# Reading the tokens in turned layout and normalizing them there, instead of normalizing and transposing them

## The chip, the core and the metric

The kernel runs on one core of one Trainium2 chip. The metric is the device time of one execution in microseconds. The core has a matrix engine (TensorE, PE in the profile; its weight loads are listed as PEld), a vector engine (VectorE, DVE), a scalar engine (ScalarE, ACT), GpSimd (POOL), and SyncE (SP), which here issues nearly all DMAs. Each engine works through its own instructions in the order in which the program wrote them, and semaphores hold an instruction until what it needs is there.

## What is computed

2048 tokens x of width 512 (32 batches of 64) attend to 2048 context tokens, each batch to its own; then comes a linear layer with a low-rank adapter. Both branches are gated and added back. Cut to what matters:

```python
x = x + tanh(g_xattn[0]) * xattn(layernorm(x), ctx, mask, bias, Wq, Wk, Wv, Wo)
x = x + tanh(g_ffn[0]) * ffn(layernorm(x), weight, bias, lora_A, lora_B, starts)

# layernorm: (x - mean) / sqrt(var + 1e-5), over the 512 features
# xattn: q = h @ Wq; k = ctx @ Wk; v = ctx @ Wv          (32 heads of 128)
#        p = softmax(q k^T / sqrt(128) + bias, masked);  out = (p v) @ Wo
```

The change touches the first layernorm only: its result, turned so that features lie on the partitions and tokens along them, is the operand of q = h @ Wq.

## The kernel before

All products of the projections are float32 made of three matmuls of split operands: a high part (a copy rounded by ACT) and a low part (the remainder, a subtraction). Projections use a seven-product scheme for a 2x2 block product: blocks p1 to p7 of the activations and of the weights are sums and differences of quarters, prepared by ACT (high part) and DVE or POOL (sums and low part).

The work is done in two passes (p = 0, 1) of 1024 tokens. A pass has three stages:

- the key stage: 16 pairs of heads (n = 0 to 15), one `unit` each; a unit is seven products of six matmuls, in the order p1, p6, p7, p5, p2, and, after the next unit's p1, its p4 and p3 (the `carry`). Keys go to DRAM (`kd`). POOL prepares the weight blocks of the next pair (`key_blocks`).
- the value stage: four groups g of four token tiles t, a unit for each, so 16 units. Values go to DRAM (`vd`). During a group POOL prepares the weight blocks of the next one (`blocks_v`) from four loads (`fetch_v`).
- attention, pair by pair: query projection, scores, softmax, product with v, output projection.

Everything beside the matmuls is written as generators ("streams"). After each product the program calls `beat()` (line 64), which takes one step of every stream; `paced(g, k)` takes a step of g every k beats. A unit has seven beats. Thus the order of instructions on every engine is fixed when the program is built; nothing is scheduled later. `drain` runs what is left of a stream.

The tokens come into this as follows. In pair 3 of the key stage `x_stats` starts: it loads the pass's eight tiles of 128 tokens (`x_load`, line 516), tokens on the partitions, and makes mean and variance of each on DVE into `mv` (128 partitions by 8 tiles by 2); `ln_rstd` then makes the reciprocal deviation `y` (128 by 8) in 15 small DVE operations. In pair 9 `x_turns` starts (line 575): it loads each tile a second time, normalizes it in place with one DVE operation (`ln_apply`, line 130), turns it by four transposes on PE into one PSUM tile (`transposes`, line 133), and ACT copies that into f (`x_turn`, line 521). f is two tiles `f0`, `f1` of 128 partitions by 4 by 512: features on the partitions, 512 tokens along each. The same memory held the turned context until pair 2. In group 2 of the value stage `turned_sums`, and in group 3 `turned_blocks`, make the seven blocks of the query projection out of f, on POOL and ACT.

Row buffers of 128 by 512 (pool `rows`) come from a ring of two; the x tiles, the mask tile, the two tiles of `turned_sums` and later the softmax's turned tiles share it. The mask (`mask_stream`, line 591) and in pass 0 the adapter masks (`adapters`, line 471) are made in group 1, and in pass 1 the reciprocal deviations of the finished pass 0 (`acc_rstd`, line 612).

The lines that matter most are the last ones of the key stage and the first ones of the value stage in `stage_a` (line 617), with the functions that it calls:

Of the kernel before, what the change touches and what calls it, by code (L numbers as in the profile page):

```python
# [9 lines left out]
F32 = mybir.dt.float32  # L10
# [4 lines left out]
ALU = mybir.AluOpType  # L15
AX = mybir.AxisListType

P = 128
D = 512
KT = D // P  # L20
# [3 lines left out]
NPH = 2  # L24
TP = NB * S // NPH
NCH = TP // 512
NT = TP // P
# [13 lines left out]


@with_exitstack
def flamingo_block(ctx: ExitStack, tc: tile.TileContext, x, ctxT, bias, mask, gx, gf,
                   wq, wk, wv, wo, wffn, bffn, la, lb, starts, out):
    nc = tc.nc
    PS = bass.MemoryType.PSUM
# [6 lines left out]
    rows = ctx.enter_context(tc.tile_pool(name="rows", bufs=2))  # L54
    st = ctx.enter_context(tc.tile_pool(name="st", bufs=2))
    dram = ctx.enter_context(tc.tile_pool(name="dram", bufs=1, space=bass.MemoryType.DRAM))
# [5 lines left out]
    streams = []  # L62
# [6 lines left out]
    def drain(g):  # L69
        if g in streams:  # L70
            streams.remove(g)
            for _ in g:
                pass
# [2 lines left out]
    make_identity(nc, ident)  # L76
    x1d = dram.tile([NT * P, D], F32, name="x1d")
    kd = [[dram.tile([P, 2, TP], F32, name=f"kd{p}_{n}") for n in range(NPR)] for p in range(NPH)]
    vd = [[dram.tile([P, NT, 512], F32, name=f"vd{p}_{g}") for g in range(2 * NG)] for p in range(NPH)]

    def big(tag, shape, dt, name):
        return slot.tile(shape, dt, tag=tag, name=name)

    def psum(name, shape=(P, 512)):
        return psp.tile(list(shape), F32, tag="ps", name=name)
# [44 lines left out]
    def ln_apply(xn, xt, mv, y, t):  # L130
        nc.vector.tensor_scalar(xn, xt, mv[:, t, 0:1], y[:, t:t + 1], ALU.subtract, ALU.mult)

    def transposes(xn, nm):
        ps = psum(f"tp{nm}", (P, KT, P))
        for kt in range(KT):
            nc.tensor.transpose(ps[:, kt, :], xn[:, kt * P:(kt + 1) * P], ident)
        return ps
# [16 lines left out]
    def sum_blocks(f, tags, nm, eng, out):  # L154
        b11, b21, b12, b22 = parts(f)
        t2 = [rows.tile([P, 512], F32, tag="row", name=f"{nm}t2_{kt}") for kt in range(2)]

        def sub(o, a, b):
            for kt in range(2):
                eng.tensor_tensor(o[kt], a[kt], b[kt], ALU.subtract)  # L160

        sub(b11, b12, b11)
        yield
        sub(b12, b22, b12)
        yield
        sub(t2, b22, b11)
        yield
        out["p6"] = act_block("p6", t2, tags, nm, eng)
        yield
        out["p7"] = act_block("p7", b12, tags, nm, eng)  # L170
        yield
        out["p5"] = act_block("p5", b11, tags, nm, eng)
        yield
        sub(b21, b21, t2)
        yield
        out["p4"] = act_block("p4", b21, tags, nm, eng)
# [275 lines left out]
    f = [big(f"f{j}", [P, KT, 512], F32, f"c0_{j}") for j in range(2)]  # L452
# [63 lines left out]
    def x_load(p, t, nm):  # L516
        xt = rows.tile([P, D], F32, tag="row", name=f"{nm}{p}_{t}")
        nc.sync.dma_start(out=xt, in_=x[p * NT + t])
        return xt

    def x_turn(xt, f, p, t):
        ps = transposes(xt, f"x{p}_{t}")
        nc.scalar.copy(f[t // 4][:, :, (t % 4) * P:(t % 4 + 1) * P], ps)

    V_ORDER = [None] * 5 + ("s3 s3 p1 p1 s2 s2 s1 p6 p6 s1 p7 p7 s4 p5 p5 p2 p2 s4 p4 p4 p3 p3").split()
    K_ORDER = "s3 s3 p1 p1 s2 s2 s1 s1 p6 p6 p5 p5 p7 p7 p2 p2 s4 s4 p4 p4 p3 p3".split()

    def paced(g, k):
        for _ in g:
            yield  # L530
            for _ in range(k - 1):
                yield
# [39 lines left out]
        mvx[p] = mv  # L572
        yield from ln_rstd(mv, f"x{p}", rx, p)

    def x_turns(p, f):
        mv, y = mvx[p], rx[p]
        xt = x_load(p, 0, "xt")
        for t in range(NT):
            nx = x_load(p, t + 1, "xt") if t + 1 < NT else None
            for _ in range(2):  # L580
                yield
            ln_apply(xt, xt, mv, y, t)
            for _ in range(3):
                yield
            x_turn(xt, f, p, t)
            xt = nx
            yield

    masks = {}

# [21 lines left out]
    def acc_rstd(p):  # L612
        for c in range(p * NCH, (p + 1) * NCH):
            yield from ln_rstd(mv2[:, c * 4:(c + 1) * 4, :], f"f{c}", rstd, c, 5)
            yield

    def stage_a(p, first, fc, res, rot, more, enter, kt0):
        xc, plain = first
        f = None
        for n in range(NPR):  # L620
            g = p * NPR + n
            if n == 0:
                sums = sum_blocks(fc, res, f"c{p}", nc.vector, xc)
                streams.append(sums)
            if n == 1:
                keys = key_blocks(p)
                streams.append(keys)
            if n == 3:
                f = [big(f"f{j}", [P, KT, 512], F32, f"xf{p}_{j}") for j in range(2)]
                t7 = big(rot[7], [P, 2, 1024], F32, f"wvr{p}_0a")  # L630
                t8 = big(rot[8], [P, 2, 1024], F32, f"wvr{p}_0b")
                fetch_v(p, 0, [t7[:, 0], t7[:, 1], t8[:, 0], t8[:, 1]])
                if more:
                    streams.append(paced(more, 2))
                xstat = x_stats(p)
                streams.append(xstat)
            if n == 5:
                vsum = [None] + [rwp.tile([P, 1024], F32, tag=f"r{2 + i}", name=f"vs{p}_0_{i}") for i in range(2)] + [None]
                v0 = paced(blocks_v(p, 0, rot, vsum, nc.vector, K_ORDER), 3)
                streams.append(v0)  # L640
            if n == 9:
                drain(xstat)
                xturn = x_turns(p, f)
                streams.append(xturn)
            kt = kt0 if n == 0 and kt0 else k_tile(g)
            w = wt[("k", g)]

            def store(kt=kt, n=n):
                for i in range(2):
                    nc.sync.dma_start(out=kd[p][n][:, i, :], in_=kt[:, i, :])  # L650
            if n < 2:
                for j in range(1 if kt is kt0 else 0, 2):
                    plain_half(w, plain, k_dst(kt), f"k{g}", j)
                store()
            else:
                if n == 2:
                    drain(sums)
                carry[:] = [unit(w, xc, None, k_dst(kt), f"k{g}", tuple(carry)), store]
        drain(xturn)
        drain(v0)  # L660
        xq = {}
        for g in range(NG):
            if g == 1:
                streams.append(mask_stream(p))
                if p:
                    streams.append(acc_rstd(p - 1))
                if p == 0:
                    streams.append(adapt)
            if g == NG - 1:
                t4 = pieces(rwp.tile([P, 1024], F32, tag="r1", name=f"x{p}t4"))  # L670
                fetch("q", p * NPR, "r0")
                bias = enter()
                streams.append(turned_blocks(f, [rot[(7 * NG + i) % 9] for i in range(7)], f"x{p}", nc.gpsimd, keep,
                                             t4, xq, bias, enter))
            for t in range(4):
                if t == 1:
                    if g + 1 < NG:
                        raw = [rwp.tile([P, 1024], F32, tag=f"r{i}", name=f"wvr{p}_{g + 1}_{i}") for i in range(4)]
                        fetch_v(p, g + 1, raw)
                        streams.append(blocks_v(p, g + 1, rot, None, nc.gpsimd, V_ORDER))  # L680
                    if g == NG - 2:
                        keep = {}
                        streams.append(turned_sums(f, f"x{p}", nc.gpsimd, keep))
                if t == 2 and g == NG - 1:
                    streams.append(prep("q", p * NPR, nc.gpsimd))
                vt = kqp.tile([P, 4, 512], F32, tag="kq", name=f"vt{p}_{g}_{t}")
                dst = {(i, j): vt[:, i * 2 + j, :] for i in range(2) for j in range(2)}
                after = unit(wt["v", p, g], xc, slice(t * P, (t + 1) * P), dst, f"v{p}_{g}_{t}", tuple(carry))

                def store(vt=vt, g=g, t=t):  # L690
                    for i in range(2):
                        for j in range(2):
                            nc.sync.dma_start(out=vd[p][2 * g + i][:, j * 4 + t, :], in_=vt[:, i * 2 + j, :])
                carry[:] = [after, store]
        enter()
        return xq
# [342 lines left out]
    for p in range(NPH):  # L1039
# [4 lines left out]
        if p < NPH - 1:  # L1044
            f, gate = [], []
# [119 lines left out]
```

## Time and profile before

| What | Value |
|---|---|
| median of 3 runs | 1545.6 us (1545.55 to 1545.87) |
| the profiled execution's own time | 1545.82 us |
| its span (first to last instruction) | 1543.8 us |
| granted TensorE clock | 1.00 |
| key stage of pass 0: start of pxk groups of pairs 8 and 9 | 90.94 and 100.90 us |
| mean DMA rate | 160 GB/s |
| DMA queue of SP and ACT (q1) | 43.6% of 16 engines |

The span counts from the first to the last recorded instruction; the time of the execution has some 2 us more around it. In a list of groups each line gives the source line, the engine, the operation, what it writes and reads by the program's names, its shape, and how often. A tile view gives the shortest, median and longest duration in ns. In the chain and in a timeline the first column is the start in us, the second the duration in us. A name such as pxk is the PSUM tile "px" of a key unit, pxv of a value unit; wk7p is a weight block of pair 7, wv_1p one of value group 1. A releaser ("<- ACT ...") is what a waiting instruction waited for.

### The profile page before, as it was taken

How to read it: one execution, taken by the hardware profiler on the slowest of the kernel's cores; microseconds unless marked ns; L12 is line 12 of the kernel's file. 1: busy time of each engine (PE TensorE's matmuls, PEld its weight loads, DVE VectorE, ACT ScalarE, POOL GpSimd, SP SyncE). 2: the span in 40 equal slices, each digit the busy share in tenths (PEclk: the TensorE clock that was granted, in tenths of full speed). 3: DMA queues.
4: the chain of work that ended last, by engine and by line, in shares of the span. 5: the costliest groups of instructions: out<-in, count | busy, mean ns of one | idle time of the engine just before them, and what ended most of it. 6: DMA issues, size and time to landing. Idle time of an engine off the chain costs nothing.

```text
span 1543.8 us, 24975 instructions
## 1 busy us (share of the span) xinstructions
PE 1535.5 (99%) x9064; PEld 1292.2 (84%) x9064; DVE 948.3 (61%) x1579; ACT 730.8 (47%) x1610; POOL 1015.8 (66%) x1128
## 2 busy tenths in 40 slices
PE   9999999999999999999999999999999999999999
PEld 7888888888888888888888888888888888888887
DVE  5665343377676757575686535437767675757774
ACT  6454233345555555556445423334555555555621
POOL 3898378967665757575589837896766575757410
PEclk9999999999999999999999999999999999999999
DMA  5654444374243424531565544437424342444211
GB/s 207 243 191 177 165 171 164 137 280 177 83 177 136 163 87 177 190 141 67 213 222 191 178 170 166 164 136 282 176 83 178 137 158 94 174 189 147 80 42 69
DMA packets 80989, 246.37 MB, mean 160 GB/s; under 512 B 9857, under 2 KB 10881, under 8 KB 72674
## 3 DMA queue, kind: packets, MB, share of 16 engines
q1 hardware_dynamic: 80578, 244.26, 43.6%
q8 instruction: 71, 1.16, 0.3%
q10 hardware_dynamic: 288, 0.52, 0.1%
q14 instruction: 52, 0.43, 0.1%
HBM read 171.35 MB, written 73.40 MB: 159 GB/s over the span
## 4 chain that ended last, share of the span: by engine, by line
PE 95%; DMA 2%; DVE 2%; POOL 0%; issue 0%; ACT 0%; SPq 0%; DVEq 0%; POOLq 0%; ACTq 0%
PE pa L97 22%; PE po L818 7%; PE pzv L97 6%; PE pvv L97 6%; PE pxv L97 6%; PE pxq L97 5%; PE pzq L97 5%; PE pxk L97 5%; PE pzk L97 5%; PE pvk L97 5%; PE pvq L97 5%; PE ps L760 4%; PE ppk L97 3%; PE pyv L97 3%; PE pf L97 3%; PE pyk L97 2%
## 5 line engine op out<-in xcount | busy, mean ns | idle before, releaser
L97 PE MATMUL pa<-wo,ch 128*128 128x512 f32 x1024 | 319.9, 393 | 0.0
L793 ACT COPY pt<-tp 32x256 f32<-32x256 f32 x496 | 200.3, 404 | 87.7 <-DVE tp L776 76.6
L89 POOL TENSOR_TENSOR wo<-rawo,wo 128x512 fp32r<-128x512 f32 x64 | 81.1, 1286 | 223.3 <-ACT wo L88 215.5
L97 PEld LDWEIGHTS pa<-wo,ch 128*128 128x128 f32 x1024 | 189.4, 188 | 40.0
L842 DVE TENSOR_TENSOR acc<-pa,acc 128x512 f32<-128x512 f32 x256 | 170.0, 673 | 79.4 <-PE pa L97 79.3
L97 PE MATMUL pa<-wo,cl 128*128 128x512 f32 x512 | 199.7, 390 | 0.0
L818 PEld LDWEIGHTS po<-pt,v 128*128 128x128 f32 x1024 | 119.1, 192 | 2.6 <-ACT pt L793 0.2
L822 DVE TENSOR_TENSOR cl<-po,ch 128x512 fp32r<-128x512 f32 x128 | 88.3, 692 | 52.5 <-ACT ch L821 52.0
L818 PE MATMUL po<-pt,v 128*128 128x128 f32 x1024 | 119.4, 275 | 0.0
L97 PEld LDWEIGHTS pa<-wo,cl 128*128 128x128 f32 x512 | 96.1, 188 | 20.7
L353 DVE TENSOR_TENSOR vt<-pvv,vt 128x512 f32<-128x512 f32 x64 | 44.1, 690 | 111.9 <-PE pvv L97 111.9
L821 ACT CAST ch<-po 128x512 fp32r<-128x512 f32 x128 | 74.8, 586 | 71.5 <-PE po L818 70.9
L766 ACT ACTIVATE sm<-sm 128x512 f32<-128x512 f32 x64 | 40.6, 634 | 123.2 <-POOL sm L765 123.2
L765 POOL TENSOR_TENSOR sm<-sm,mx 128x512 f32<-128x512 f32 x64 | 66.9, 1048 | 46.8 <-DVE mx L764 46.8
L375 ACT COPY vt<-pxv 128x512 f32<-128x512 f32 x32 | 18.8, 588 | 132.1 <-PE pxv L97 132.1
L353 DVE TENSOR_TENSOR kT<-pvk,kT 128x512 f32<-128x512 f32 x56 | 38.5, 688 | 67.1 <-PE pvk L97 66.7
L721 POOL TENSOR_TENSOR sm<-sm,madd 128x512 f32<-128x512 f32 x60 | 76.3, 1292 | 2.6 <-DMA sm<-bias 2.6
L784 POOL TENSOR_TENSOR sm<-sm,r 128x512 f32<-128x512 f32 x64 | 66.8, 1044 | 14.5 <-DVE r L783 11.1
L353 DVE TENSOR_TENSOR qT<-pzq,qT 128x512 f32<-128x512 f32 x64 | 44.3, 692 | 38.0 <-PE pzq L97 37.4
L760 PE MATMUL ps<-kB,qT 128*64 128x64 f32 x2048 | 67.2, 224 | 0.3 <-DVE qT L353 0.3
L353 DVE TENSOR_TENSOR vt<-pzv,vt 128x512 f32<-128x512 f32 x64 | 44.2, 691 | 37.1 <-PE pzv L97 36.9
L760 PEld LDWEIGHTS ps<-kB,qT 128*64 128x64 f32 x2048 | 62.5, 138 | 4.9 <-issue 0.7
(978 smaller groups left out, 3704.0 us busy)
## 6 DMA issues: line engine op xcount, KB each, us to landing
kd<-kT SPq DMA_DIRECT2D x64, 512.0 KB, 3.6
vd<-vt SPq DMA_DIRECT2D x128, 256.0 KB, 2.3
kB<-kd SPq DMA_DIRECT2D x32, 1024.0 KB, 4.9
v<-vd SPq DMA_DIRECT2D x32, 1024.0 KB, 8.7
rawq<-wq SPq DMA_DIRECT2D x32, 512.0 KB, 4.0
sm<-bias SPq DMA_DIRECT2D x64, 256.0 KB, 5.3
rawo<-wo SPq DMA_DIRECT2D x32, 512.0 KB, 3.4
rawk<-wk SPq DMA_DIRECT2D x31, 512.0 KB, 5.4
```

What stands on the lines that cost most here:

```text
L89: eng.tensor_tensor(lo, raw, hi.bitcast(F32), ALU.subtract)
L97: nc.tensor.matmul(ps, a, b, start=start and i == 0, stop=stop and i == 3 * n - 1, skip_group_check=True)
L353: nc.vector.tensor_tensor(o, ps, i, ALU.add)
L721: nc.gpsimd.tensor_tensor(t, t, masks[p][0], ALU.add)
L760: nc.tensor.matmul(ps[h * S:(h + 1) * S, t, :], qT[:, i, tok], kT[:, i, tok], start=True, stop=True)
L765: nc.gpsimd.tensor_tensor(s, s, mx.unsqueeze(2).to_broadcast([P, NT, S]), ALU.subtract)
L784: nc.gpsimd.tensor_tensor(ss[i], ss[i], r.unsqueeze(2).to_broadcast([P, NT, S]), ALU.mult)
L793: f(pt[dst, i, :, src], of[src, :, ki * 32:(ki + 1) * 32])
L818: nc.tensor.matmul(ps[:, t * P:(t + 1) * P], b["v", n // 2][c][:, t, hg * P:(hg + 1) * P], pt[:, i, c * 4 + t, :], start=True, stop=True)
L821: nc.scalar.copy(ch[:, i, sl], ps)
L822: nc.vector.tensor_tensor(cl[:, i, sl], ps, ch[:, i, sl].bitcast(F32), ALU.subtract)
L842: nc.vector.tensor_tensor(acc[t], ps, acc[t], ALU.add)
```

## The change

The host passes x a second time, as `xT`, in the layout of f. Two loads per pair in pairs 6 to 9 put the raw, turned tokens into f. In pair 10 `x_spread` stores the means and the reciprocal deviations to DRAM, so that they lie in the order of the tokens there (`lnd`, two rows of 1024 numbers; partition q of tile t goes to place t*128 + q). From the start of the value stage `x_norm`, at one step in two beats, loads 512 means and 512 deviations at a time onto all partitions and normalizes f in place on DVE: a subtraction and a multiplication for each of the eight rows of 512. The second loads of x, `ln_apply` on them, the transposes and ACT's copies are gone from this place. `mask_stream` and `adapters` start in group 2 instead of group 1, `acc_rstd` stays in group 1.

```diff
+    lnd = [dram.tile([2, TP], F32, name=f"lnd{p}") for p in range(NPH)]
...
-    def x_turn(xt, f, p, t):
-        ps = transposes(xt, f"x{p}_{t}")
-        nc.scalar.copy(f[t // 4][:, :, (t % 4) * P:(t % 4 + 1) * P], ps)
...
-    def x_turns(p, f):
+    def x_spread(p):
         mv, y = mvx[p], rx[p]
-        xt = x_load(p, 0, "xt")
-        for t in range(NT):
-            nx = x_load(p, t + 1, "xt") if t + 1 < NT else None
-            for _ in range(2):
-                yield
-            ln_apply(xt, xt, mv, y, t)
+        nc.sync.dma_start(out=lnd[p][0].rearrange("(t q) -> q t", q=P), in_=mv[:, :, 0])
+        nc.sync.dma_start(out=lnd[p][1].rearrange("(t q) -> q t", q=P), in_=y)
+
+    def x_norm(p, f):
+        for j in range(NCH):
+            row = [rows.tile([P, 512], F32, tag="row", name=f"ln{p}_{j}_{i}") for i in range(2)]
+            for i in range(2):
+                nc.sync.dma_start(out=row[i], in_=lnd[p][i][j * 512:(j + 1) * 512].partition_broadcast(P))
             for _ in range(3):
                 yield
-            x_turn(xt, f, p, t)
-            xt = nx
-            yield
+            for op, r in ((ALU.subtract, row[0]), (ALU.mult, row[1])):
+                for kt in range(KT):
+                    nc.vector.tensor_tensor(f[j][:, kt, :], f[j][:, kt, :], r, op)
+                    yield
...
-            if n == 9:
+            if 6 <= n < 6 + KT:
+                for j in range(NCH):
+                    nc.sync.dma_start(out=f[j][:, n - 6, :], in_=xT[p * NCH + j, n - 6])
+            if n == 10:
                 drain(xstat)
-                xturn = x_turns(p, f)
-                streams.append(xturn)
+                x_spread(p)
...
-        drain(xturn)
         drain(v0)
+        xnorm = paced(x_norm(p, f), 2)
+        streams.append(xnorm)
         xq = {}
         for g in range(NG):
-            if g == 1:
+            if g == 1 and p:
+                streams.append(acc_rstd(p - 1))
+            if g == 2:
+                drain(xnorm)
                 streams.append(mask_stream(p))
-                if p:
-                    streams.append(acc_rstd(p - 1))
                 if p == 0:
                     streams.append(adapt)
...
+        "xT": C(A(x).reshape(NPH * NCH, 512, KT, P).transpose(0, 2, 3, 1)),
```

More of the change, by code (lines that the diff above doesn't have):

```diff
@@ L43, in flamingo_block @@
 @with_exitstack
-def flamingo_block(ctx: ExitStack, tc: tile.TileContext, x, ctxT, bias, mask, gx, gf,
+def flamingo_block(ctx: ExitStack, tc: tile.TileContext, x, xT, ctxT, bias, mask, gx, gf,
                    wq, wk, wv, wo, wffn, bffn, la, lb, starts, out):
```

## The prediction

> **What bounds the kernel now.** I read the shares of busy time first, then the waits of TensorE, then the chain of work through the end of the key stage, where the change takes instructions out.
>
> ```profile
> span 1543.8 us, 24975 instructions
> PE 1535.5 (99%) x9064; PEld 1292.2 (84%) x9064; DVE 948.3 (61%) x1579; ACT 730.8 (47%) x1610; POOL 1015.8 (66%) x1128
> ```
> ```profile
> PE warm L457 <- POOL ident masks.py:199: 1.3, 1, 1.3
> PE pt L993 <- DVE fa L985: 1.0, 1, 1.0
> ```
>
> PE is busy in 1535.5 of 1543.8 us; its longest waits are 1.3 and 1.0 us, both far from here. So the kernel is a queue of matmuls: one that is taken out shortens the span by its slot, one engine's relief elsewhere gives nothing. The tile view of the transposes' PSUM tile and the chain show what a slot is:
>
> ```profile
> L136 PE MATMUL tpx<-ident,xt x64: 270/272/273, 100.3 to 893.9; 128*128 128x128 f32 x64
> L523 ACT COPY xf<-tpx x16: 572/587/593, 101.5 to 894.2; 128x512 f32<-128x512 f32 x16
> L131 DVE TENSOR_SCALAR xt<-xt,mv,yx x16: 531/957/961, 97.6 to 890.3; 128x512 f32<-128x512 f32 x16
> ```
> ```profile
> 90.94 2.72 PE pxk L97 x12
> ...
> 99.10 1.36 PE pzk L97 x6
> 100.46 0.44 PE tpx L136 x4
> 100.90 2.77 PE pxk L97 x12
> ```
>
> The 272 ns of one transpose overlap in the pipeline: a group of four stands in the chain with 0.44 us. From one pair of p2/p1 products to the next (pxk) it is 9.52 us without transposes and 9.96 with a group in between.
>
> **What the change removes.** 64 transposes, 16 ACT copies, 16 DVE applies, 16 loads of x. Only the transposes lie on the path. Their price comes from the chain: pxk starts at 90.94, and the eighth interval ends at pxv 170.96, so 80.02 us for eight units of 9.52 (76.16): 3.86 us for eight groups, 0.48 each. In the second pass 823.72 to 903.74 is 80.02 too. Sum: 2 x 3.86 = 7.72 us. ACT's 16 x 0.587 and DVE's 16 x 0.81 lie beside PE and count nothing.
>
> **Added: eight loads of turned x per pass** (256 KB, two per pair in pairs 6 to 9). As many bytes as the loads removed. In SP's order each two follow the previous weight load (issued at 60.64, 69.90, 79.73, 88.56) and stand ahead of the key store that waits for the pair's end some 8 us later. Their destination, the tiles of f, was last read before pair 2, so SP waits for nothing there. With a store (1 MB), a weight load (0.5 MB) and these 0.5 MB a pair moves 2 MB in 9.52 us, 220 GB/s; slices near 100 us moved 391. Nothing, while that holds; if it didn't, a late weight load has the 6.4 us below.
>
> **Added: the spread of the moments.** Two stores per pass of 1024 runs of 4 bytes each. The trace has no such transfer. SP issues them right after pair 11's weight load, at about 99 us; the rstd they wait for was ready at 90.5. Behind them on SP: pair 9's key store (issued at 108.25) and the weights of pair 12 (109.14). The stretches of DMA share after that place (columns: stretch, us, PE, PEld, DVE, ACT, POOL, clock, DMA share, GB/s):
>
> ```profile
> 102.40:104.40 2.00, 2.00 (x10) 1.66 (x9) 0.00 (x0) 1.47 (x4) 1.49 (x3) 1.00 0.56 194
> 104.40:106.40 2.00, 2.00 (x10) 1.67 (x9) 1.33 (x2) 1.38 (x4) 1.68 (x3) 1.00 0.03 8
> 106.40:108.40 2.00, 2.00 (x10) 1.65 (x10) 2.00 (x4) 0.19 (x1) 1.84 (x3) 1.00 0.00 0
> ```
>
> The DMA engines are empty for 4 us. What overshoots delays pair 12's weights. There ACT's cast ran at 114.51 and POOL's remainder was done at 115.7; PE took block p1 of that pair at 122.16. So 4 + 6.4 = 10.4 us are free in a pass. (kd_9's landing also holds the next kT buffer; ACT's copy into it, at 114.03, may slip behind it, but the accumulator is reused only 7 us later.)
>
> Bounds of the cost: the nearest row is the LoRA load, 512 runs of 192 bytes, 32 per DMA engine. In its stretch (1431 to 1432 us, share 1.01) 268 KB moved where 418 to 434 moved just before; 98 KB of them are its own, the other 170 take 0.40 us at 426 GB/s, so 0.60 us for 32 runs, 19 ns each. Other end: its landing took 5.5 us, the mask's 2.7, so 2.8 us for 32 runs, 88 ns. The spread has 128 runs per engine in both stores together: 2.4 to 11.2 us. The Trainium skill (DMA: Bandwidth & Descriptors, section Rules for kernel authors) warns of exactly this, one descriptor per element where the last dimension is strided; its own measured floor (section Bandwidth) is about 10.5 ns a packet, which as an estimate would make 1.3 us. The price is below the free 10.4 us by the page and by the first row, 0.8 us above it by the second. I take the lower row, 2.4 us, because the stretch measures throughput and the landing includes a queue of other loads; hence 0, with up to 1.6 us in two passes for the range. The issue itself cost SP 0.32 to 1.41 us for 128 runs of other sizes; if it grew eightfold from 0.33, 5.3 us for both, SP would still be free before 108.25.
>
> **Added: four broadcast loads** (256 KB) per pass. The first two stand on SP ahead of the last key store and are issued some 8 us before DVE wants them; loads of that size land in 4 to 7 us. The second two wait on SP for DVE's last multiply of the first half; behind them stand only value stores, whose buffers come round two units (19 us) later. They too have three paced yields, 8 us. Nothing.
>
> **Added: 16 subtracts and multiplies per pass on DVE** (128x512, both inputs in SBUF), one in two beats (2.72 us) over value groups 0 and 1. DVE's nearest rows of this form take 0.69 alone and up to 1.3 beside POOL. In two beats DVE has at most two PSUM adds (0.69 each) and one of these: 1.38 + 1.3 = 2.68, within 2.72. In the second pass the small rstd operations come in too (12.8 us for 30 between 932 and 985, 0.43 each, one a beat): a unit of seven beats then asks 3.45 for adds, 3.0 for these and 3.5 to 4.6 for the new ones, 10.0 to 11.0 in 9.52, so over two such units DVE may trail by 1 to 3 us. PE reuses pv and pz three products (4.1 us) after they are filled, and an add needs 0.69, so a lag up to 3.4 is free. I take 0, with 1 us for the range.
>
> **What these do to POOL.** POOL makes the value weights of the next group meanwhile, and slows when DVE reads two SBUF inputs:
>
> ```profile
> 67.99 0.74 POOL L298 TENSOR_TENSOR wk7p<-rawk,wk7p 128x256 fp32r<-128x256 f32 x1
> 68.69 1.19 POOL L298 TENSOR_TENSOR wk6p<-rawk,wk6p 128x256 fp32r<-128x256 f32 x1
> ...
> 207.19 2.73 POOL L187 TENSOR_TENSOR wv_1p<-vs,wv_1p 128x512 fp32r<-128x512 f32 x2
> 209.88 0.15 POOL L498 IOTA bi<- 128x32 int32 x1
> ```
>
> A clash costs POOL 0.45 us. Group 1's blocks run from 177 to 209.92 on POOL; PE takes the last, p3, at 212.96, so 3.0 us slack. Some eight of the new operations fall between 183 (until there POOL waits for ACT anyway, 3.36 us) and 210: 8 x 0.45 = 3.6, less 1.3 us of POOL's own gaps, 2.3 late: no stall. The Trainium skill (SBUF — State Buffer, Who interferes with whom) speaks against the change more strongly: whoever issues second is blocked for the other's whole instruction. By that rule 8 x 0.69 - 1.3 = 4.2, 1.2 over the slack, 2.4 us in two passes. I take the row. POOL then has 5.2 us idle for the next load, so nothing carries over.
>
> **Moved: mask, adapters** one group later, with the same distance to the weight loads on SP and the same 1.1 us lag of POOL's iota. POOL's first two turned sums may wait 1.4 us for the mask's row buffer, then idle for weights anyway. The adapters' wait for a small load held DVE 2.8 us without a stall of PE; it keeps that length. Nothing.
>
> Sum on the profiled execution: 1545.82 (span 1543.8 and 2.0 around it) - 7.72 = 1538.1. The median of the runs is 0.2 lower: **1537.9 us**.
>
> **Rivals.**
> A, the likeliest: the slots go, nothing stalls, 1537.3 to 1539.5 (chance 0.70).
> B, POOL or DVE trails in groups 0 and 1: 2.4 us by the rule above and 1 us of DVE's lag, 1537.9 + 3.4 = about 1541.3; for it, the 3.0 us slack is the thinnest cover here; against it, the row's 0.45 us. Chance 0.10 for 1539.5 to 1542.5.
> C, slower: the 4-byte runs. It decides from 10.4 + 3.86 = 14.3 us per pass on, 111 ns a run. If the LoRA load's whole landing were run time, 5.5/32 = 172 ns, the spread takes 22 us, overshoots by 11.6, and each pass loses 7.7 net: 1561. For it: nothing shows 4-byte stores to DRAM; against: the stretch with 19 ns. Chance 0.12 for a time beyond 1548.7; a smaller overshoot, between 1542.5 and that, 0.04.
> D, the transposes hid a POOL bound: then a pair stays at 10.0 us and the time at 1545.6. Against: POOL's last operation of pairs 6 to 9 starts at 69.83, 78.72, 87.69, 96.42, so 8.9 us a pair, under 9.52. Chance 0.02; with C's smaller overshoot, 0.06 lies within 0.2%.
> Below 1537.3: 0.02.
>
> 0.2% is 3.1 us, about what a measurement can tell from no change: faster means under 1542.5. Faster 0.82 (A, B, below), same 0.06, slower 0.12. Range 1537.0 to 1545.0: A, B, most of what lies below A, and about half of what lies within 0.2%, some 0.84 in all.
>
> **What would show it.** pxk intervals of 9.52 throughout pairs 9 to 15; the first pxv group 3.9 us earlier; no PE wait for ACT or POOL there. If C: a wait of ACT's cast of pair 12 for its weights, and DMA busy with few GB/s after 99 us. If B: waits of PE for wv_1 near its p4 and p3. If the spread's two stores land later than 14 us after issue, the forecast is wrong.

## The result and the profile after

| | before | after |
|---|---|---|
| median | 1545.63 us (1545.55 to 1545.87, 6 runs) | 1539.13 us (1537.70 to 1540.29, 6 runs) |
| ratio to before | | 0.9957, interval 0.9944 to 0.997 |
| profiled execution: own time, span | 1545.82, 1543.8 us | 1539.96, 1538.0 us |

The change makes the kernel 6.5 us faster, 0.43%. The forecast was 1537.9 in 1537.0 to 1545.0. The executions no longer lie close together: three of the six at 1537.70 to 1538.30, three at 1539.96 to 1540.29. What separates these groups is the question of the experiments.

The head of the page of after, and its chain of work at the end of pass 0's key stage (start, duration):

```profile
span 1538.0 us, 24845 instructions
PE 1528.1 (99%) x9000; PEld 1286.0 (84%) x9000; DVE 963.8 (63%) x1595; ACT 721.2 (47%) x1594; POOL 1019.3 (66%) x1128
```
```profile
90.83 2.72 PE pxk L98 x12
...
100.35 2.72 PE pxk L98 x12
...
109.87 2.72 PE pxk L98 x12
```

PE has 64 instructions and 7.4 us of busy time less; the interval of pxk is 9.52 us without exception in this stage, where before had 9.96 to 10.04 whenever a group of transposes stood in it. The first pxv group starts at 166.99 (170.96 before). So the slots went as forecast. The waits of PE in the same execution show one that before does not have:

```profile
PE pyk L98 <- POOL wk27p L299: 1.3, 1, 1.3
PE warm L458 <- POOL ident masks.py:199: 1.3, 1, 1.3
PE pt L998 <- DVE fa L990: 1.0, 1, 1.0
```

wk27p is the weights of pair 11 of pass 1. The chain of work, followed back from that matmul, and the timelines of SP and ACT there:

```profile
826.84 12.24 DMA rawk<-wk
...
845.20 1.15 POOL wk27p L299
846.35 0.04 issue
846.39 1.20 PE pyk L98 x4
...
850.31 2.72 PE pxk L98 x12
```
```profile
826.84 0.74 SPq L264 DMA_DIRECT2D rawk<-wk  x1
827.63 1.19 SPq L575 DMA_DIRECT2D lnd<-mv  x1
828.86 0.93 SPq L576 DMA_DIRECT2D lnd<-yx  x1
```
```profile
839.11 0.41 ACT L295 CAST wk27p<-rawk 128x256 fp32r<-128x256 f32 x1 [6.49 <-DMA rawk<-wk]
```

The load of pair 11's weights (rawk) was issued 0.8 us ahead of the two stores of the moments, and it landed 12.24 us after its issue; the median of such loads in this execution is 5.4 us. ACT's first cast of it waited 6.49 us, POOL's remainders came late behind it, and PE's p6 of that pair waited. In pass 0 of the same execution the cast waited 2.93 us, and PE not at all. The table of DMA issues (the last figure is the median time from issue to landing) has the stores:

```profile
rawk<-wk SPq DMA_DIRECT2D x31, 512.0 KB, 5.4
...
lnd<-mv SPq DMA_DIRECT2D x2, 4.0 KB, 13.6
lnd<-yx SPq DMA_DIRECT2D x2, 4.0 KB, 12.6
```

4 KB take 13.6 us to land, and 512 KB take 5.4. The stretches of pass 0, with the DMA share and GB/s in the last two columns:

```profile
102.00:104.00 2.00, 2.00 (x10) 1.69 (x9) 0.04 (x1) 1.22 (x3) 1.37 (x2) 1.00 0.95 92
104.00:106.00 2.00, 2.00 (x10) 1.65 (x10) 1.47 (x3) 0.00 (x0) 0.00 (x0) 1.00 0.05 0
106.00:108.00 2.00, 2.00 (x11) 1.65 (x10) 1.21 (x2) 1.33 (x4) 0.85 (x2) 1.00 0.97 96
108.00:110.00 2.00, 2.00 (x11) 1.65 (x10) 1.39 (x3) 0.21 (x1) 1.92 (x3) 1.00 0.78 27
110.00:112.00 2.00, 2.00 (x11) 1.65 (x10) 0.59 (x1) 1.13 (x3) 1.92 (x4) 1.00 0.82 37
```

DMA is busy with few GB/s, the sign that the prediction named for its slow rival C, but with a stretch of nothing at 104 to 106 us, while the stores have not landed. ACT and POOL stand empty in just that stretch: they wait for pair 11's weights.

### The profile page after: what moved, and what is told of

It reads as the page before. It is cut to its first block, busy times and chain, and to the rows that moved or that the text cites. A ratio compares the mean times of both kernels' runs of the same rounds, so it can differ in the third digit from the quotient of the medians.

```text
span 1538.0 us, 24845 instructions
## 1 busy us (share of the span) xinstructions
PE 1528.1 (99%) x9000; PEld 1286.0 (84%) x9000; DVE 963.8 (63%) x1595; ACT 721.2 (47%) x1594; POOL 1019.3 (66%) x1128
## 4 chain that ended last, share of the span: by engine, by line
PE 93%; DMA 3%; DVE 2%; POOL 1%; issue 1%; ACT 0%; SPq 0%; ACTq 0%; DVEq 0%; POOLq 0%
PE pa L98 22%; PE po L823 7%; PE pzv L98 6%; PE pvv L98 6%; PE pxv L98 6%; PE pzq L98 5%; PE pxq L98 5%; PE pvq L98 5%; PE pzk L98 4%; PE pvk L98 4%; PE pxk L98 4%; PE ps L765 4%; PE pyv L98 3%; PE ppk L98 3%; PE pf L98 3%; PE pyq L98 2%
## 5 line engine op out<-in xcount | busy, mean ns | idle before, releaser
L354 DVE TENSOR_TENSOR qT<-pvq,qT 128x512 f32<-128x512 f32 x64 | 44.1, 690 | 35.5 <-PE pvq L98 35.5
```

Source lines behind the costliest of these rows:

```text
L354: nc.vector.tensor_tensor(o, ps, i, ALU.add)
```

## The experiments

The theory after this comparison: the removed slots give the full 7.72 us, all other additions are hidden, and the stores of the moments hold DMAs that are in flight or follow (pair 11's weights, the key store of pair 9), which costs 2 us in some executions. The rivals: the loss comes from the value stage (DVE and POOL, B in the prediction), or from SP's queue being blocked by the issue of the stores. Where a median of before stands with an experiment, it is that of its own chip and hour.

**The changed kernel, unaltered**, on the chip of the three experiments that follow.

> The changed kernel unaltered, as the mark for the three others on the same chip. My theory: the two stores of 4-byte runs hold up the weights of pair 11 (6.5 us of waiting in pass 1 of the profiled execution), PE then waits 1.3 to 2 us or not at all, by how long the stores take in that execution; so the times lie between 1537.7 and 1540.3, and the whole spread is this wait. Rival: the shortfall of 1 to 2 us lies in the value stage, where DVE's new operations slow POOL; then the wait for pair 11 would be seen without any effect on the time.

Measured: 1539.14 us (1537.96 to 1540.42, 5 runs), before 1545.74; ratio 0.9956 (0.9944 to 0.9969). Its profiled execution is one of the short ones, 1537.96 with a span of 1535.9, and PE waits for no key weights in it. Cast waits for rawk: 3.0 us in pass 0, none in pass 1. There the two pxk groups around pair 11 of pass 1 start at 838.77 and 848.29, 9.52 apart; in the profiled execution above the second one starts at 850.31. So that one wait costs PE 2.0 us in all (1.35 of it as a gap), which is about the distance of the two groups of executions.

**Without the stores** (the rows of means and deviations are loaded from x instead, so the normalization uses wrong numbers; the work is the same otherwise).

```diff
-        nc.sync.dma_start(out=lnd[p][0].rearrange("(t q) -> q t", q=P), in_=mv[:, :, 0])
-        nc.sync.dma_start(out=lnd[p][1].rearrange("(t q) -> q t", q=P), in_=y)
...
-                nc.sync.dma_start(out=row[i], in_=lnd[p][i][j * 512:(j + 1) * 512].partition_broadcast(P))
+                nc.sync.dma_start(out=row[i], in_=x[p * NT + j][i].partition_broadcast(P))
```

> The two stores of the moments are left out, and the broadcast rows are read from x instead, so the normalization uses wrong numbers; all else stays. My theory: pair 11's weights land in about 5 us, PE doesn't wait, 1537.9 in every run, with a scatter like that of the kernel before (0.3 us). Rival (value stage): 1538 to 1540 as with the stores.

Measured: 1537.88 us (1537.83 to 1538.35), ratio 0.9949 (0.9936 to 0.9961). The longest cast wait for the weights of pair 11 of either pass is this one (wk27p is pair 11 of pass 1):

```profile
832.94 0.41 ACT L295 CAST wk27p<-rawk 128x256 fp32r<-128x256 f32 x1 [0.35 <-DMA rawk<-wk]
```

Four of the five executions are within 0.11 us. The 1.3 us between the medians of this and the unaltered kernel, and most of the scatter, belong to the stores.

**The stores in long runs**: PE turns the moments (two small transposes and an ACT copy per pass), and each store then has 8 runs of 512 bytes.

```diff
...
+        for i, m in enumerate((mv[:, :, 0], y)):
+            nc.tensor.transpose(ps[0:NT, i, :], m, ident)
+        tm = st.tile([NT, 2, P], F32, tag="tm", name=f"tms{p}", bufs=1)
+        nc.scalar.copy(tm, ps[0:NT])
+        for i in range(2):
+            nc.sync.dma_start(out=lnd[p][i].rearrange("(t q) -> t q", q=P), in_=tm[:, i, :])
```

> The moments are first turned on PE (two transposes of 128x8 a pass) and stored in 16 runs of 512 bytes instead of 2048 of 4. My theory: no wait for pair 11's weights; PE pays some 0.1 to 0.25 us a pass for the transposes, so 1538.1 to 1538.4 with little scatter, and the stores land in 2 to 4 us. Rival: if it is not the count of runs but the wait on DRAM that holds the queue, the stores still take over 8 us and the time stays at 1538 to 1540.

Measured: 1538.41 us (1538.32 to 1539.90), ratio 0.9952 (0.9938 to 0.9965). No cast waits for pair 11's weights in either pass, and the key stores cost ACT 1.8 us of waiting in all, 0.9 at most. This kernel issues its stores at 104.30, later than the changed kernel (98.74), so that pair 11's weights go free proves nothing about the length of the runs; the key store behind them does: it lands 3.4 us after its issue, as without stores, where behind stores of 4-byte runs that were issued between 101 and 107 us it took 7.8 to 13.0 us (three of the kernels below). When the stores landed, the profile does not show. That the median is 0.5 us over the kernel without the stores is the transposes: the one pxk interval with the two of them in it is 0.26 us longer in pass 0 and 0.25 in pass 1.

The profiled execution is the longest of the five, 1539.90, though nothing waits for the stores in it. It lost its time at the very start, in the first products. They are shown here for this execution and then for that of the kernel without the stores:

```profile
5.34 24.30 PE ppk L98 x96
```
```profile
5.12 23.06 PE ppk L98 x96
```

So not every long execution is the stores' doing: the start alone can cost some 1.5 us (0.22 of it before these products), and a long execution without a profile can be either.

**The stores in pair 15** instead of pair 10, where no weight load of a key pair follows or precedes.

```diff
             if n == 10:
                 drain(xstat)
+            if n == NPR - 1:
                 x_spread(p)
```

> The same stores five pairs later, ahead of pair 15's unit, when no more key weights are fetched. My theory: nothing waits for key weights; the broadcast rows are issued only when the stores have landed (some 14 us later) and DVE's first new operation may wait a few us for them, with its value adds behind it; PE tolerates about 3.4 us of that. 1537.9, or up to 3 us a pass more if the rows come too late. Rival (value stage): as the unaltered kernel.

Measured: 1538.28 us (1537.69 to 1538.90), ratio 0.995 (0.9938 to 0.9963). The stores still take 12.6 us to land (issued at 146.03, the rows are fetched at 158.77). What they hold is the last key store: ACT's first value copies wait 2.4 us for it, PE for nothing.

**Four stores instead of two** (the second two to memory that nothing reads).

```diff
+        nc.sync.dma_start(out=lne[p][0].rearrange("(t q) -> q t", q=P), in_=mv[:, :, 0])
+        nc.sync.dma_start(out=lne[p][1].rearrange("(t q) -> q t", q=P), in_=y)
```

> The two stores of 4-byte runs are made twice (the second time into DRAM that nobody reads). My theory: the price goes with the number of runs, about 6 us for each store, so the four stores are done some 25 us after their issue instead of 13; pair 11's weights are held no longer than before if they were only caught between the first stores, but the key store of pair 9 and the weights of pair 12 now land some 10 us late, and PE stalls 4 to 8 us in each pass: 1546 to 1554. Rival (a fixed latency of such a store, not its runs): 1538 to 1541 as with two stores.

Measured: 1550.12 us (1549.75 to 1551.34), before 1545.78; ratio 1.0029 (1.0017 to 1.0041): slower than before. The size is as expected, the place is not. The waits of PE and of ACT in the profiled execution (the longest, 1551.34):

```profile
PE pxk L99 <- ACT kT L360: 7.2, 2, 5.1
```
```profile
ACT kT L360 <- DMA kd<-kT: 17.1, 4, 10.0
ACT wk27p L296 <- DMA rawk<-wk: 5.4, 1, 5.4
ACT wk11p L296 <- DMA rawk<-wk: 2.8, 1, 2.8
```

ACT's copy of pair 10's keys waits 10.0 us for the key store of pair 9, because it needs that buffer (kT); PE's pxk needs the accumulator that ACT has not emptied. Pair 12's weights, which the prediction watched, cost 0.6 us of waiting. And a long wait of PE has a second price, seen in the column of the granted clock (after the six figures of the engines):

```profile
120.00:122.00 2.00, 0.00 (x0) 0.00 (x0) 0.00 (x0) 0.00 (x0) 0.00 (x0) 1.00 0.92 260
122.00:124.00 2.00, 0.00 (x0) 0.00 (x0) 0.00 (x0) 0.25 (x1) 0.00 (x0) 0.94 1.04 424
124.00:126.00 2.00, 1.61 (x4) 1.33 (x5) 0.83 (x2) 1.43 (x4) 0.61 (x1) 0.50 1.02 416
126.00:128.00 2.00, 2.00 (x7) 1.54 (x6) 1.90 (x4) 0.45 (x2) 1.86 (x3) 0.50 0.09 37
128.00:130.00 2.00, 2.00 (x6) 1.63 (x5) 0.66 (x2) 0.41 (x1) 1.89 (x2) 0.50 0.79 260
```

After 5 us without matmuls the clock is 0.50 for at least 6 us, and six matmuls take 2.9 us instead of 1.5.

**The kernel before, with only the stores added**, in pair 10.

```diff
+            if n == 10:
+                mv, y = mvx[p], rx[p]
+                nc.sync.dma_start(out=lnd[p][0].rearrange("(t q) -> q t", q=P), in_=mv[:, :, 0])
+                nc.sync.dma_start(out=lnd[p][1].rearrange("(t q) -> q t", q=P), in_=y)
```

> The kernel before with the two stores of the moments added at pair 10, which nobody reads; transposes and all else stay. My theory: the stores take some 13 us here too and hold pair 11's weights by 3 to 7 us, but with a pair at 10.0 us instead of 9.52 POOL is further ahead, so PE stalls at most 1 us a pass: 1545.6 to 1547. If the stores cost nothing by themselves: 1545.6 with the scatter of the kernel before.

Measured: 1545.84 us (1545.62 to 1546.16, 13 runs), before 1545.78; ratio 1.0 (0.9992 to 1.0008). The same two stores cost nothing here. A load of x stands ahead of them on SP, so they are issued 3.0 us after pair 11's weight load instead of 0.8, and no cast waits for it:

```profile
98.34 0.46 SPq L264 DMA_DIRECT2D rawk<-wk  x1
100.91 0.33 SPq L519 DMA_DIRECT2D xt<-x  x1
101.30 0.43 SPq L648 DMA_DIRECT2D lnd<-mv  x1
```

The key store behind them does come late, by 3.8 us at ACT's copy, which PE does not feel.

**The stores from ACT's queue.**

```diff
-        nc.sync.dma_start(out=lnd[p][0].rearrange("(t q) -> q t", q=P), in_=mv[:, :, 0])
-        nc.sync.dma_start(out=lnd[p][1].rearrange("(t q) -> q t", q=P), in_=y)
+        nc.scalar.dma_start(out=lnd[p][0].rearrange("(t q) -> q t", q=P), in_=mv[:, :, 0])
+        nc.scalar.dma_start(out=lnd[p][1].rearrange("(t q) -> q t", q=P), in_=y)
```

> The two stores are issued from ACT's queue instead of SP's, at the same place in the order of the program. My theory: if the earlier issued weights of pair 11 are held because they share SP's rings with the stores, they now land in 5 us and PE doesn't wait: 1537.9 to 1538.5, less about 2 us in which ACT issues. Rival: the DMA engines themselves or DRAM are held by the small runs; then the weights are late just as with SP and the time scatters up to 1540 or more, since ACT loses 2 us for the issue ahead of its casts.

Measured: 1538.45 us (1537.96 to 1538.68), ratio 0.9952 (0.9938 to 0.9965). Pair 11's cast does not wait; the key store of pair 9 of pass 1 is late by 4.3 us, without a wait of PE. But ACT reached the stores only at 101.78, so the queue and the moment were changed together; a later experiment parts them.

**Without stores, row loads and normalization** (f stays unnormalized: neither means nor deviations are applied).

```diff
-        nc.sync.dma_start(out=lnd[p][0].rearrange("(t q) -> q t", q=P), in_=mv[:, :, 0])
-        nc.sync.dma_start(out=lnd[p][1].rearrange("(t q) -> q t", q=P), in_=y)
...
-        xnorm = paced(x_norm(p, f), 2)
-        streams.append(xnorm)
```

> Stores of the moments, broadcast loads and the 32 DVE operations on f are all left out, so that the tokens go into the projection without normalization. My theory: the DVE operations and the broadcast loads are fully hidden, so this is no faster than the kernel that lacks the stores alone: 1537.8 to 1538.0. Rival (value stage): faster than that by 0.5 to 2 us.

Measured: 1537.75 us (1537.71 to 1537.80), ratio 0.9948 (0.9935 to 0.996). That is 0.13 us below the kernel without the stores alone, measured on another chip. The traces leave even less. From the first pxv group of pass 0 to the first pxk group of twelve in pass 1, a stretch that holds the value stage with all its additions, it is 595.63 us here (167.11 to 762.74), 595.66 without the stores alone, 595.60 in after and 595.64 in before. So 32 DVE operations, eight broadcast loads and their effect on POOL cost nothing that can be measured. Rival B is refuted.

**The stores behind a small copy on DVE**, one step later, to put a distance between them and the weight load.

```diff
...
+        yield
+        mc = st.tile([P, 2, NT], F32, tag="mc", name=f"mc{p}", bufs=1)
+        nc.vector.tensor_copy(mc[:, 0], mv[:, :, 0])
+        nc.vector.tensor_copy(mc[:, 1], y)
+        for i in range(2):
+            nc.sync.dma_start(out=lnd[p][i].rearrange("(t q) -> q t", q=P), in_=mc[:, i])
...
-                x_spread(p)
+                streams.append(x_spread(p))
```

> The two stores are issued some 6 us later than in the changed kernel (at about 104.8 us instead of 98.7), behind a small DVE copy of the moments in pair 10; by then the weights of pair 11 have landed. Theory 1: only what is on its way when the stores come, or follows at once, is held; the weights of pair 11 are then free, but pair 9's key store, issued 1.8 us after them, lands when the stores are done (about 118 us), ACT waits for it with its copy into that buffer and PE may wait for the accumulator: 1538 to 1541. Theory 2: only weights matter; then 1537.9 with little scatter.

Measured: 1547.63 us (1547.20 to 1550.09, 13 runs), before 1545.67; ratio 1.0016 (1.0008 to 1.0024). That is 6.6 us above the range of theory 1, the most telling miss. The copy ran later than meant, so the stores were issued at 106.62, right ahead of pair 9's key store (107.72) and pair 12's weights (108.81). Pair 11's weights are on time, as wished, and both of the others are not:

```profile
121.48 0.59 ACT L359 COPY kT<-pxk 128x512 f32<-128x512 f32 x1 [9.47 <-DMA kd<-kT]
122.66 0.41 ACT L295 CAST wk12p<-rawk 128x256 fp32r<-128x256 f32 x1 [0.59 <-DMA rawk<-wk]
```
```profile
122.12 1.66 PE L98 MATMUL pxk<-c0p,wk11p 128*128 128x512 f32 x6 [2.88 <-ACT kT L359]
...
130.41 1.84 PE L98 MATMUL pyk<-c0p,wk12p 128*128 128x512 f32 x4 [1.35 <-POOL wk12p L299]
```

The key store came free 13.8 us after its issue, the weights 13.9, both about 15 to 16 us after the stores' issue at 106.62. ACT's copy then stands late, in pass 1 by 8.8 us as well, and PE waits 2.9, 1.35 and 2.2 us; after the second and the third of these waits the granted clock is down as well:

```profile
124.00:126.00 2.00, 1.98 (x10) 1.36 (x9) 1.90 (x4) 0.20 (x1) 1.92 (x3) 1.00 0.21 86
...
132.00:134.00 2.00, 2.00 (x6) 1.56 (x5) 0.69 (x1) 0.38 (x1) 2.00 (x4) 0.50 0.79 315
...
858.00:860.00 2.00, 2.00 (x7) 1.54 (x6) 1.16 (x3) 1.54 (x4) 1.40 (x2) 0.50 0.92 375
```

This profiled execution is one of the longer ones (1549.48); eight of the 13 lie between 1547.2 and 1547.8. Against the kernel without the stores the same 8 KB per pass cost 0 to 3 us at 98.74 and some 10 us eight microseconds later.

**One store per pass** (the deviations' rows are loaded from x, so the multiplication uses wrong numbers).

```diff
-        nc.sync.dma_start(out=lnd[p][1].rearrange("(t q) -> q t", q=P), in_=y)
...
```

> Only the store of the means is made; the row of deviations is read from x, so the multiplication uses wrong numbers. By the line through two stores (13.6 us from first issue to last landing) and four (some 23), one store should land in 8 to 9 us. My theory: pair 11's weights are held less, by 2 to 3 us at most, and PE never waits: 1537.8 to 1538.4, without the runs near 1540. Rival (one store is enough to hold the queue): scatter up to 1540 as with two.

Measured: 1537.95 us (1537.83 to 1539.40), before 1545.67; ratio 0.9951 (0.9939 to 0.9964). The time is as expected, the landing is not: one store alone takes 14.4 us to land in pass 0 and 12.8 in pass 1, as long as two. Pair 11's cast does not wait in pass 0 and 0.6 us in pass 1; the key store is late by 3.7 us. One of the five executions took 1539.40; it has no profile, so whether the stores or the start made it long is not known.

**The changed kernel again**, on the chip of the last two.

> The changed kernel once more, on the same chip as the two others, to count how often it comes near 1540: by the first two sets about half of the runs at 1539.1 to 1540.4, the rest at 1537.7 to 1538.3.

Measured: 1540.58 us (1539.71 to 1541.08, 6 runs), ratio 0.9967 (0.9955 to 0.9979). All six executions are long here, not half of them. On this same chip one store (1537.95) gave five executions of which four are short. The profiled one, the shortest of the six, has the wait again, at the same place; what makes the others up to 1.4 us longer still has no profile:

```profile
PE pyk L98 <- POOL wk27p L299: 1.4, 1, 1.4
```
```profile
ACT wk27p L295 <- DMA rawk<-wk: 6.2, 1, 6.2
```

**The stores from ACT's queue, but early**: as the experiment on ACT's queue, three ACT instructions sooner, so that little but the queue differs from the changed kernel.

```diff
     def x_spread(p):
+        for _ in range(4):
+            yield
...
+            if n == 9:
+                streams.append(x_spread(p))
             if n == 10:
                 drain(xstat)
-                x_spread(p)
```

> The two stores stay on ACT's queue but stand three ACT instructions earlier, behind the middle cast of pair 10, so that they should be issued at about 99.5 us instead of 101.8, some 1.5 us after pair 11's weight load, which is still in flight. If what holds that load is the nearness in time (the stores share the DMA engines with it), ACT's cast of pair 11 waits 2 us or more for rawk again, as in the changed kernel (2.9 us), and the median is 1538.3 to 1540. If it is the shared queue of SP, the cast of pair 11 does not wait (under 0.5 us), the key store of pair 9 does as before (4 us), and the median is 1537.9 to 1538.5.

Measured: 1537.93 us (1537.90 to 1539.53, 5 runs), before 1545.68; ratio 0.9952 (0.9939 to 0.9966). ACT's timeline of pass 0:

```profile
99.23 0.39 ACTq L577 DMA_DIRECT2D lnd<-mv  x1
99.72 0.70 ACTq L578 DMA_DIRECT2D lnd<-yx  x1
...
106.20 0.41 ACT L295 CAST wk11p<-rawk 128x256 fp32r<-128x256 f32 x1 [2.37 <-DMA rawk<-wk]
```

The weight load was issued on SP at 98.07, the stores 1.2 us later on another engine's queue, and the load is held all the same: the cast waits 2.37 us, and the load took 8.1 us to land where it took 5.7 without the stores. The profile counts ACT's DMAs under another queue than SP's (q1): it is q10, which has 288 packets in after and 4448 here.

```profile
q10 hardware_dynamic: 4448, 0.54, 0.3%
```

So a shared queue is not needed to hold the load; nearness in time is what is left. This rests on one pass: in pass 1 the cast waits 0.76 us, where it waits 0.35 without the stores. PE has no wait in this execution; the median expected for that case (1538.3 to 1540) was too high.

## Why the prediction held, and which steps were wrong

**The removed slots: right, to 0.1 us.** The first pxv group of pass 1, in before and in the profiled execution of the unaltered kernel without a stall:

```profile
903.74 2.72 PE pxv L97 x12
```
```profile
895.89 2.72 PE pxv L98 x12
```

That is 7.85 us earlier than before; 0.13 of it was there at pair 8 already (90.81 against 90.94). The remaining 7.72 is the sum of the prediction. Without the stores the whole kernel takes 1537.88, where 1537.9 was forecast.

**The additions of the value stage: right.** They cost nothing that can be measured. The clash on POOL is the row's 0.45 us: in after a pair of POOL's weight operations takes 2.54 us where none of DVE's new operations falls on it, 2.99 or 3.04 with one and 3.44 with two. The last pair below meets a second one only at its very end.

```profile
185.95 3.44 POOL L188 TENSOR_TENSOR wv_1p<-vs,wv_1p 128x512 fp32r<-128x512 f32 x2
...
190.60 2.54 POOL L188 TENSOR_TENSOR wv_1p<-vs,wv_1p 128x512 fp32r<-128x512 f32 x2
...
201.09 2.99 POOL L188 TENSOR_TENSOR wv_1p<-wvr,wv_1p 128x512 fp32r<-128x512 f32 x2
204.04 2.99 POOL L188 TENSOR_TENSOR wv_1p<-vs,wv_1p 128x512 fp32r<-128x512 f32 x2
```

The last of them ends at 207.03 and PE takes the block at 208.98: 1.95 us of slack, where the step left 0.7 (3.0 less 2.3) and the rule of the Trainium skill (SBUF — State Buffer, Who interferes with whom: the one that issues second waits for the other's whole instruction) would have left less than none. The loads of turned x, the broadcast loads, the lag of DVE and the moved mask cost nothing that shows.

**The stores of the moments: wrong in the price and in the victim.** The step "I take the lower row, 2.4 us, because the stretch measures throughput" failed. From the first issue (98.74) to the last landing are 13.8 us in pass 0 (by the medians), and with two further stores the last landing is 21 to 23 us behind the first issue. The upper row, 11.2 us from the LoRA load's landing, was near; the skill's warning against such stores (DMA: Bandwidth & Descriptors, Rules for kernel authors) was right in kind, and the estimate from its floor, 1.3 us, ten times too low; the page measured that floor on loads issued from GpSimd, not on stores. By the prediction's own test (stores that land later than 14 us make the forecast wrong) they stayed just inside, 13.9 us at most in after.

The step "What overshoots delays pair 12's weights" failed too. It counted only DMAs that are issued behind the stores. Held were pair 11's weights, already in flight, and pair 9's key store. Their cover is shorter than the 10.4 us that was counted: with the stores later (from ACT's queue), pair 11's cast runs at 103.65; in pass 0 of after it ran at 106.67 and PE lost nothing; in pass 1 it ran at 839.11, which is 110.2 on pass 0's scale (pass 1's products run 728.9 later), and PE lost 2.0. So some 4.5 us are free there. The key store was set aside with "the accumulator is reused only 7 us later"; with four stores, and in the kernel with the copy on DVE, this was the wait that decided.

So the range held because the delay of pair 11's weights (in the six profiled passes of the changed kernel from nothing to 6.5 us) crosses its 4.5 us in one pass at most and by 2 us only. The shortfall of the median is 1.2 us of 7.7. That the range held is in part luck: the prediction priced the stores at 2.4 us and found no harm in them, and the same argument would have found none in them eight microseconds later, where 2.4 us still fit ahead of the 6.4 us of pair 12's weights. There the same mechanism, rival C's, was 10 us strong and took back the whole gain.

**What stays open.** Why the DMA engines show nothing for about 2 us amid one or two stores; why one store takes as long to land as two; why the same stores at the same place hold the weights by 6.5 us in one pass and not at all in another, and on one chip more than on another. No trace shows what inside the DMA engines or the memory does the holding. Why the start of an execution is sometimes 1.5 us longer is open too. The placement in pair 15, the stores on ACT's queue (later and earlier) and the long runs gave 1538.28, 1538.45, 1537.93 and 1538.41, against 1539.14 and 1540.58 of the changed kernel; all beat before, but their lead over the changed kernel is not larger than its own scatter between chips.

## What to carry to other kernels

On a full engine, a slot taken out comes back one to one, so a small edit elsewhere decides whether it is kept. A DMA of many tiny runs is priced by the landing of such a transfer, not by the bytes or by the throughput of a better one, and it must be held against everything in flight near it: the load issued just before, and the store behind it whose buffer somebody needs. Move it to where none of these is awaited within about 15 us, or make its runs long.

## What the runs showed of the hardware

- Two stores of 1024 runs of 4 bytes (8 KB) took 10.7 to 13.9 us each to land, one alone 12.8 and 14.4; 512 KB in long runs take 5.4. In after the DMA engines show a share of 0.05 (pass 0) and 0.00 (pass 1) for about 2 us of this.
- A load that was issued 0.8 us earlier can be held by them: 12.24 us to land in one pass, no delay in another. From another engine's queue 1.2 us later they held it in one pass of two (8.1 us to land).
- They can also hold the issue of what follows: the two DMAs of the next key store took SP 0.81 us in after, and 4.08 and 3.27 us in pass 0 of the kernels with the early stores on ACT's queue and with the stores added to before.
- After 5 us without matmuls the clock was granted at 0.50 for at least 6 us. Shorter gaps were not alike: after one of 2.9 us it stayed at 1.00, after one of 1.35 some 7 us later it was 0.50 in one stretch of 2 us, and after a single one of 2.2 us in pass 1 too.
